# Four unread products of 512 columns after each image's part of the filter matrices, in the forward sums of a two-layer MetaFormer kernel

## The chip, the cores and the metric

The kernel runs on one core of one Trainium2 chip. A core has five engines that run side by side, each through its own queue in order: TensorE (PE in the profile; its weight loads are shown as PEld), VectorE (DVE), ScalarE (ACT), GpSimd (POOL) and SyncE (SP), which here issues the DMA transfers. TensorE writes its results to PSUM, from where ScalarE and VectorE fetch them. The metric is the device time of one execution in microseconds; the median of several runs counts.

## The reference

Two layers work on x of shape (8, 128, 32, 32). Each layer has a first part over the map and a second part over the 1024 tokens of an image, with a norm ahead of each and the input added behind it. Layer 0 has attention and then a spectral filter; layer 1 has a deformable convolution and then a mixture of experts. Only the spectral filter bears on the change. In the reference, cut to it:

```python
def _stu_conv(phi, u, n):
    Vf = jnp.fft.rfft(phi, n=n, axis=0)
    Uf_p = jnp.fft.rfft(u, n=n, axis=1)
    Uf_m = jnp.fft.rfft(u * sgn3, n=n, axis=1)
    U_plus = jnp.fft.irfft(Vf[None, :, :, None] * Uf_p[:, :, None, :], n=n, axis=1)[:, :sl]
    U_minus = jnp.fft.irfft(Vf[None, :, :, None] * Uf_m[:, :, None, :], n=n, axis=1)[:, :sl]
...
out = jnp.einsum('btkd,k,kde->bte', U_plus, s, Mpp)
out = out + jnp.einsum('btkd,k,kde->bte', U_minus, s, Mpm)
```

Each of the 8 images (u: 1024 tokens of 128 channels, normalised) is convolved along its tokens with 16 filters phi, and multiplied by one 128x128 matrix for each filter (`Mpp`, `Mpm`). That is done for four lengths of the sequence, and one of the four results is chosen by `log_weights + gumbel`.

## The kernel before

The program has four stages: attention (to about 900 us of the span), the forward sums (900 to 1038), the products in the frequency domain (to about 1400), and then the way back, the convolution and the experts.

**The forward sums** are `Spectral.forward` (L1718). They turn each image into its spectrum by products with a table of cosines and sines, `t`: 128 tokens by 4 residues by 2 pieces by 512 columns, float32, made at the start by `table` (L1704). The loop at L1794 runs over the images b = 0 to 7 and issues, in this order:

- `image(b)` (L1920): for each parity, `halves` (L1873) makes two sums in two PSUM buffers `p_half`, of two products each (L1882), so eight products of 128x128 by 128x512 for an image. ScalarE copies the second sum of each pair to `other` (L1888), and `both` (L1891) lets VectorE add and subtract the pair into `us`. After them TensorE turns the image, two times four 128x128 transposes into `p_t` (L1933), and ScalarE copies each of these to `ut` (L1934).
- the load of image b + 4 (SP), the store of `us` to `ud` and of `ut` to `utd` (L1937, L1940, SP), the load of a piece of the filter matrices for b + 3 (SP), and the norm of image b + 3 (L66): statistics on VectorE, seventeen small operations on POOL for the inverse root, and eight normalising activations on ScalarE (L105).
- `parts(b)` (L1907): four products of 512 columns in four strips of the array give this image's piece of the filter matrices in `p_a` (L1912); ScalarE (even b) or VectorE (odd b) copies it to `a`.
- at b = 1 also `spectra` (L1897), the spectrum of the filters, eight products through the same `halves`; at b = 5 and 6 the tables for the way back; and each time four steps of the setup of layer 1 (`fill`).

Everything here stands in the order in which it is written (`manual_schedule`). Each engine takes its instructions in that order and waits on semaphores for what others make.

**The PSUM buffers** are in one pool (L1694): `wide` (L1698) gives one of six buffers of 512 columns, to `p_half`, `p_a` and later `p_g`; `small` (L1701) gives one of two, to `p_t` and later `p_z`. A buffer is given again when its last reader has finished. `halves` needs four `wide` buffers for an image and `parts` one, so that TensorE can start on the next image while the earlier one waits to be fetched, until the six are used up.

**Behind the loop**, `generate` (L1944) makes the filter matrices of a chunk of frequencies from all of `a` and `v` (`p_g`, L1951), `products` (L2020) loads the spectra of all images again from `ud` (`uc`, L2030), `stationaries` (L1960) lays them out (`at`, on POOL and VectorE for the first chunk), and `apply` (L1992) multiplies (`p_z`, L2000).

Of the kernel before, what the change touches and what calls it, by code (L numbers as in the profile page):

```python
# [19 lines left out]
B = 8  # L20
# [45 lines left out]
def layer_norm_pieces(nc, pool, src, dst, eps):  # L66

    t = {}  # L70

    def stats(i):
        if i == 0:
            for name, shape in (
                ("st", [P, NT, 6]), ("mv", [P, NT, 2]), ("v", [P, NT]), ("y", [P, NT]),
                ("w", [P, NT]), ("nm", [P, NT]),
            ):
                t[name] = pool.tile(shape, F32, tag=f"lp_{name}", name=f"lp_{name}")
        nc.vector.bn_stats(t["st"][:, i, :], src()[:, i, :])
        nc.vector.bn_aggr(t["mv"][:, i, :], t["st"][:, i, :])  # L80

    def inverse(n):

        v, y, w, mv = t["v"], t["y"], t["w"], t["mv"]
        bits = [i.bitcast(I32) for i in (y, v)]
        ops = [
            lambda: nc.gpsimd.tensor_scalar(v, mv[:, :, 1], eps, None, ALU.add),
            lambda: nc.gpsimd.tensor_scalar(bits[0], bits[1], -0.5, 0x5F3759DF, ALU.mult, ALU.add),
            lambda: nc.gpsimd.tensor_scalar(v, v, -0.5, None, ALU.mult),
        ]  # L90
        ops += 3 * [
            lambda: nc.gpsimd.tensor_mul(w, y, y),
            lambda: nc.gpsimd.tensor_mul(w, w, v),
            lambda: nc.gpsimd.tensor_scalar(w, w, 1.5, None, ALU.add),
            lambda: nc.gpsimd.tensor_mul(y, y, w),
        ]
        ops += [
            lambda: nc.gpsimd.tensor_mul(t["nm"], mv[:, :, 0], y),
            lambda: nc.gpsimd.tensor_scalar(t["nm"], t["nm"], -1.0, None, ALU.mult),
        ]  # L100
        for op in ops[2 * n : 2 * n + 2]:
            op()

    def norm(i):
        nc.scalar.activation(  # L105
            dst()[:, i, :], src()[:, i, :], AF.Identity, bias=t["nm"][:, i : i + 1],
            scale=t["y"][:, i : i + 1],
        )

    return (  # L110
        [partial(stats, i) for i in range(NT)] + [partial(inverse, n) for n in range(9)]
        + [partial(norm, i) for i in range(NT)]
    )
# [656 lines left out]
class Plan:  # L770
# [18 lines left out]
    def unread(self, gap):  # L789

        return min(8, int((gap - 0.7) * 0.7 / 0.427 + 0.5)) if gap > 0.7 else 0
# [871 lines left out]
class Spectral:  # L1663
# [54 lines left out]
    def forward(self, ctx, fill, head):  # L1718


        nc = self.nc
        sb = ctx.enter_context(self.tc.tile_pool(name="s_fwd", bufs=2))
        one = ctx.enter_context(self.tc.tile_pool(name="s_one", bufs=1))
        self.sb = sb

        room = self.first.rearrange("p a b -> p (a b)")
        used = 0

        def early(size):
            nonlocal used  # L1730
            used += size
            return room[:, used - size : used]

        u = [head.x] + [one.tile([P, NT, C], F32, name=f"u{n}") for n in range(1, 4)]
        u += u

        def load(b):
            head.load(u[b], b)

        pieces = []  # L1740

        def load_parts(n):
            m = sb.tile([P, 16, C], F32, tag="m", name="m", bufs=3)
            for rows, src in ((slice(0, 64), self.M_plus), (slice(64, 128), self.M_minus)):
                nc.sync.dma_start(
                    m[rows], src[:, :, 16 * n : 16 * n + 16, :].rearrange("f k d e -> (f k) d e")
                )
            pieces.append(m)

        self.angles = [  # L1750
            [early(2 * LOW).bitcast(I32).rearrange("p (a f) -> p a f", a=2) for _ in range(2)]
            for _ in range(2)
        ]
        phi = early(HT)[0 : 2 * NF]
        load(1)
        nc.sync.dma_start(phi[0:NF], self.phi_e[:, PHI_PAD : PHI_PAD + HT])
        nc.sync.dma_start(phi[NF : 2 * NF], self.phi_o[:, PHI_PAD + 1 : PHI_PAD + 1 + HT])
        load_parts(0)
        load(2)
        load_parts(1)  # L1760
        load(3)
        mus = early(NFR * TAPS * C).rearrange("d (f i e) -> d f i e", f=NFR, i=TAPS)
        for f in range(NFR):
            nc.sync.dma_start(mus[:, f], self.M_u[f].rearrange("i d e -> d i e"))
        load_parts(2)

        self.shift = one.tile([P, 1], F32, name="shift")
        nc.gpsimd.memset(self.shift, -PI)
        waves = one.tile([P, 2], F32, name="at_wave")
        nc.gpsimd.iota(waves, pattern=[[2 * P, 2]], base=1, channel_multiplier=2,  # L1770
                       allow_small_or_imprecise_dtypes=True)
        times = early(4 * QT).rearrange("p (r q) -> p r q", r=4)
        nc.gpsimd.iota(times, pattern=[[1, 4], [4, QT]], base=0, channel_multiplier=0,
                       allow_small_or_imprecise_dtypes=True)
        t = one.tile([P, 4, 2, 2, LOW], F32, name="t")
        back = early(4 * 2 * 2 * QT).rearrange("p (r i a q) -> p r i a q", r=4, i=2, a=2)
        self.lags = early(4 * 2 * 8 * NF).rearrange(
            "p (r i j a k) -> p r i j a k", r=4, i=2, j=4, a=2
        )

        def norm(b):
            return layer_norm_pieces(nc, sb, lambda: u[b], lambda: u[b], 1e-5)

        for r in (0, 2, 1, 3):
            for i in range(2):
                self.table(t[:, r, i], head.odd, head.at[:, r, i : i + 1])
        for piece in norm(1):
            piece()
        self.scales(one)
        self.filters_turned(one, phi)  # L1790
        for piece in norm(2):
            piece()

        for b in range(B):  # L1794
            store = self.image(b, u[b], t)
            if b + 4 < B:
                load(b + 4)
            store()
            if b + 3 < B:
                load_parts(b + 3)  # L1800
                for piece in norm(b + 3):
                    piece()
            self.parts(b, pieces[b])
            if b == 1:
                self.spectra(t)
            if b == 2:
                for f in range(NFR):
                    by = self.weights[:, f : f + 1]
                    if f == 0:
                        nc.vector.tensor_scalar(self.mu, mus[:, f], by, None, ALU.mult)  # L1810
                    else:
                        nc.vector.scalar_tensor_tensor(
                            self.mu, mus[:, f], by, self.mu, ALU.mult, ALU.add
                        )
            if b in (5, 6):
                for r in range(2 * b - 10, 2 * b - 8):
                    for i in range(2):
                        self.table(back[:, r, i], times[:, r, :], waves[:, i : i + 1])
                half = slice(8 * QT * (b - 5), 8 * QT * (b - 4))
                nc.sync.dma_start(  # L1820
                    self.backd[:, half], back.rearrange("p r i a q -> p (r i a q)")[:, half]
                )
            for _ in range(4):
                next(fill, None)
        for _ in fill:
            pass
# [70 lines left out]
    def spectra(self, t):  # L1897

        for par in range(2):
            one, other = self.halves(  # L1900
                par, lambda r, i: self.lags[:, r, i].rearrange("p j a k -> p (j a k)"), t
            )
            self.both(
                lambda half, cs: self.v[:, :, LC * half : LC * half + LC, 2 * par + cs], one, other
            )

    def parts(self, n, m):  # L1907
# [325 lines left out]
```

## Time and profile before

| what | value |
|---|---|
| median of 3 runs | 1879.45 us (1876.2 to 1879.82) |
| the profiled execution | 1878.91 us, of which 1877.2 us are the span from first to last instruction |
| busy in the span: PE, DVE, ACT, POOL | 1673.7, 1385.4, 1052.6, 1156.8 us |
| mean granted TensorE clock | 0.953 of full speed |

By stage, from the windows of the trace (us busy):

| window (us) | PE | DVE | ACT | POOL | granted clock | DMA share |
|---|---|---|---|---|---|---|
| 0 to 900, attention | 851.29 | 717.14 | 576.16 | 665.39 | 0.99 | 0.04 |
| 900 to 1037.8, forward sums | 95.19 | 68.03 | 54.03 | 34.76 | 0.83 | 0.79 |
| 1037.8 to 1063.2, first filter matrices | 17.25 | 18.15 | 13.96 | 12.92 | 1.00 | 0.33 |
| 1063.2 to 1400, products | 321.51 | 187.72 | 148.86 | 124.70 | 0.98 | 0.32 |
| 1400 to 1877.2, way back, convolution, experts | 388.45 | 394.36 | 259.54 | 319.05 | 0.90 | 0.59 |

How to read the profile. A row of the timeline gives the start (us from the span's start), the length (us), the engine, the line of the kernel, the operation, what it writes and reads with its shape, how many instructions are merged, and in brackets the idle time of the engine just ahead of them with what ended it. A float32 product is shown as two rows: the eight `p_half` products of an image count as x16. In the row of slices the span is cut in 40 equal parts; each digit is a busy share in tenths, and PEclk is the clock that TensorE was granted, in tenths of full speed. "issue" in the chain of waits is time for which the profile shows no releaser.

### The profile page before, as it was taken

To read this page: it belongs to the slowest core of one execution; us is meant where nothing else is said; L and a number is where in the kernel's file an instruction comes from. 1 tells how busy PE (TensorE), PEld (TensorE's weight loads), DVE (VectorE), ACT (ScalarE), POOL (GpSimd) and SP (SyncE) were. 2 spreads that over 40 slices of the span, in tenths; PEclk is the share of its full clock that TensorE was granted. 3 is DMA by queue.
4 is the path that set the end of the run, shared out by engine and by line. 5 is a ranking of instruction groups with operands and counts; after the bars stand their busy time and mean duration, and the time that the engine had idled before them with its cause. 6 is when DMAs were issued, how large, how long until landed. Compare 5 with 4: busy or idle time off the path is not lost.

```text
span 1877.2 us, 51680 instructions
## 1 busy us (share of the span) xinstructions
PE 1673.7 (89%) x22228; PEld 1024.7 (55%) x22228; DVE 1385.4 (74%) x2107; ACT 1052.6 (56%) x1676; POOL 1156.8 (62%) x1215
## 2 busy tenths in 40 slices
PE   5999999999999999998587899999888497888788
PEld 3545555555555555554133688888665363555555
DVE  2778787888888787888545666666158888999883
ACT  3666766666666666665324455555145655666630
POOL 3778777787778777786231345445126768888740
PEclk9999999999999999999688999999898588999989
DMA  1000000000000000000678322222568775855620
GB/s 30 13 2 24 2 2 24 2 24 2 24 2 24 2 2 24 2 13 2 143 176 226 122 62 71 58 62 60 183 194 262 229 223 152 237 176 164 206 83 20
DMA packets 157999, 156.17 MB, mean 83 GB/s; under 512 B 15424, under 2 KB 136864, under 8 KB 156352
## 3 DMA queue, kind: packets, MB, share of 16 engines
q1 hardware_dynamic: 142400, 102.41, 19.3%
q0 software_dynamic: 15360, 50.34, 8.7%
q8 instruction: 177, 2.90, 0.7%
q14 instruction: 62, 0.51, 0.1%
HBM read 96.39 MB, written 56.33 MB: 81 GB/s over the span
## 4 chain that ended last, share of the span: by engine, by line
PE 55%; DVE 15%; POOL 9%; ACT 8%; issue 8%; DMA 4%; SPq 2%; DVEq 0%; POOLq 0%; ACTq 0%
PE s L598 13%; PE av L650 9%; PE p_g L1951 6%; PE z L619 5%; PE p_z L2000 5%; ACT e L603 5%; PE rb L633 3%; PE p_out L1413 3%; DVE ga L1403 3%; POOL t L612 2%; DVE g L1310 2%; DMA g<-tab,idx 2%; PE pq L554 2%; PE p_mix L1245 1%; DVE e L640 1%
## 5 line engine op out<-in xcount | busy, mean ns | idle before, releaser
L612 POOL TENSOR_TENSOR t<-e 128x1024 f32<-128x1024 f32 x256 | 608.4, 2377 | 192.4 <-ACT e L603 190.2
L603 ACT ACTIVATE e<-s 128x2048 f32<-128x2048 f32 x256 | 481.0, 1879 | 261.5 <-PE s L598 254.3
L640 DVE TENSOR_TENSOR e<-e,rb 128x2048 f32<-128x2048 f32 x256 | 568.6, 2280 | 70.0 <-PE rb L633 68.6
L598 PE MATMUL s<-q,k 32*128 32x256 f32 x4096 | 299.0, 406 | 25.4 <-ACT e L603 21.2
L650 PE MATMUL av<-e,vt 128*32 128x256 f32 x4096 | 290.6, 392 | 2.9 <-DVE e L640 1.7
L1288 POOL DMA_INDIRECT g<-tab,idx x192 | 199.4, 1038 | 133.7 <-ACT cn_m L1508 67.5
L598 PEld LDWEIGHTS s<-q,k 32*128 32x128 f32 x4096 | 187.9, 187 | 153.1 <-ACT e L603 139.6
L1295 ACT ACTIVATE g<-g,w 128x128 f32<-128x128 f32 x604 | 186.2, 390 | 61.2 <-DMA g<-tab,idx 48.9
L1976 POOL TENSOR_SCALAR at<-uc 128x256 f32<-128x256 f32 (+2 forms) x62 | 75.3, 1216 | 174.1 <-issue 86.4
L626 DVE RECIPROCAL r<-z 128x256 f32<-128x256 f32 x64 | 112.5, 1757 | 94.1 <-PE z L619 94.1
L650 PEld LDWEIGHTS av<-e,vt 128*32 128x32 f32 x4096 | 102.0, 110 | 134.9 <-issue 82.6
L1951 PE MATMUL p_g<-v,a 32*128 32x128 f32 x4096 | 159.5, 285 | 9.4 <-ACT ga L1683 3.7
L1951 PEld LDWEIGHTS p_g<-v,a 32*128 32x128 f32 x4096 | 132.4, 187 | 38.3 <-issue 23.0
L1413 PE MATMUL p_out<-ga,ew 128*128 128x512 f32 x256 | 128.0, 646 | 16.4 <-DVE ga L1403 16.3
L619 PE MATMUL z<-t,group 128*32 128x256 f32 x2048 | 122.2, 379 | 0.0
L1685 DVE COPY gb<-p_g 128x512 f32<-128x512 f32 x128 | 82.4, 685 | 46.9 <-PE p_g L1951 46.2
L1685 DVE COPY ga<-p_g 128x512 f32<-128x512 f32 x128 | 82.4, 685 | 44.0 <-PE p_g L1951 44.0
L1683 ACT COPY gb<-p_g 128x512 f32<-128x512 f32 x128 | 68.7, 589 | 69.9 <-PE p_g L1951 69.1
L1683 ACT COPY ga<-p_g 128x512 f32<-128x512 f32 x128 | 68.7, 589 | 66.7 <-PE p_g L1951 66.7
L1403 DVE TENSOR_TENSOR ga<-p_g,tc 128x2048 f32<-128x2048 f32 x32 | 73.1, 2283 | 31.6 <-PE p_g L1394 31.6
L1413 PEld LDWEIGHTS p_out<-ga,ew 128*128 128x128 f32 x256 | 50.5, 206 | 76.4 <-issue 56.5
L619 PEld LDWEIGHTS z<-t,group 128*32 128x32 f32 x2048 | 66.4, 110 | 44.2 <-issue 0.3
(309 smaller groups left out, 2378.6 us busy)
## 6 DMA issues: line engine op xcount, KB each, us to landing
tab<-hx SPq DMA_DIRECT2D x24, 512.0 KB, 5.1
tab<-hx SPq DMA_DIRECT2D x72, 128.0 KB, 5.9
ud<-us SPq DMA_DIRECT2D x8, 1024.0 KB, 6.4
uc<-ud SPq DMA_DIRECT2D x16, 512.0 KB, 4.4
yd<-zs SPq DMA_DIRECT2D x32, 256.0 KB, 3.0
ga<-yd SPq DMA_DIRECT2D x32, 256.0 KB, 3.5
xc<-in_x SPq DMA_DIRECT2D x8, 512.0 KB
x1d<-xt SPq DMA_DIRECT2D x8, 512.0 KB, 3.8
```

The lines of the kernel that those rows point to most:

```text
L598: nc.tensor.matmul(s[:, j, c, :], img["k"][rows, 2 * r + c, :], q[rows, qc * QU : (qc + 1) * QU], start=True, stop=True,)
L603: nc.scalar.activation(e.rearrange("p j c q -> p (j c q)"), s.rearrange("p j c q -> p (j c q)"), AF.Exp, scale=float(HD) ** -0.5,)
L612: nc.gpsimd.tensor_add(t, e[:, :, 0, :], e[:, :, 1, :])
L619: nc.tensor.matmul(un["z"][32 * j : 32 * j + 32, 0:QU], group, un["t", r][:, j, :], start=(r == 0), stop=(r == 3), skip_group_check=True,)
L640: nc.vector.tensor_tensor(e, e, un["rb"].unsqueeze(2).to_broadcast([P, NH, 2, QU]), ALU.mult)
L650: nc.tensor.matmul(qrt["av"][32 * j : 32 * j + 32, 0:QU], img["v"][:, 2 * r + c, P * hg + 32 * j : P * hg + 32 * j + 32], un["e", r][:, j, ...
L1288: nc.gpsimd.indirect_dma_start(out=t["g", i][:, tap].rearrange("p k c -> p (k c)"), out_offset=None, in_=rows, in_offset=bass.IndirectOffs ...
L1295: nc.scalar.activation(t["g", i][:, tap, k, :], t["g", i][:, tap, k, :], AF.Identity, scale=t["w"][:, i, tap, k : k + 1],)
L1413: nc.tensor.matmul(t["out"], self.ew[:, first + e, :], xg[:, e, :], start=(first + e == 0), stop=(first + e == NE - 1), skip_group_check=True,
L1683: self.nc.scalar.copy(dst, src)
L1685: self.nc.vector.tensor_copy(dst, src)
L1951: nc.tensor.matmul(banks[j][:, i * P : (i + 1) * P], self.a[rows, 4 * n + i, :], self.v[rows, ch].rearrange("p f k -> p (f k)"), start=Tru ...
```

## The change

Behind `parts(b)` the loop calls a new function for each image but the last. It takes one of the two `small` buffers and writes four products to it, with the identity as the fixed operand and the first 512 columns of the table `t` as the moving one. Nothing reads the result.

```diff
@@ -1801,6 +1801,8 @@
                 for piece in norm(b + 3):
                     piece()
             self.parts(b, pieces[b])
+            if b + 1 < B:
+                self.unread(t)
             if b == 1:
                 self.spectra(t)
             if b == 2:
@@ -1902,6 +1904,14 @@
             )
             self.both(
                 lambda half, cs: self.v[:, :, LC * half : LC * half + LC, 2 * par + cs], one, other
+            )
+
+    def unread(self, t):
+        p = self.small("p_idle")
+        for _ in range(4):
+            self.nc.tensor.matmul(
+                p, self.ident, t[:, 0, 0].rearrange("p a f -> p (a f)"), start=True, stop=True,
+                skip_group_check=True,
             )
 
     def parts(self, n, m):
```

## The prediction

> **What bounds the kernel now.** I read the page's slices first, to find where TensorE is neither busy nor at full clock:
>
> ```profile
> PE   5999999999999999998587899999888497888788
> PEclk9999999999999999999688999999898588999989
> DMA  1000000000000000000678322222568775855620
> ```
>
> The change sits in slices 19 to 22 (a slice is 46.9 us). There TensorE is idle for part of the time, its granted clock falls to 0.6, and the DMA engines are the busiest of the span. The windows view gives this stage, from 900 to 1037.8 us: PE 95.2 of 137.8 us busy, DVE 68.0, ACT 54.0, POOL 34.8, clock 0.83. No engine fills the stage; a chain that passes from engine to engine sets its length. The chain of waits follows it over the stage: the seventeen small POOL operations of a layer norm, then "issue" of about 10 us, then POOL again, once each 15 us. ScalarE's part of the timeline shows one such round:
>
> ```profile
> 1013.58 3.18 ACT L105 ACTIVATE u<-u,lp_nm,lp_y 128x128 f32<-128x128 f32 x8 [9.55 <-POOL lp_nm L99]
> 1016.67 0.56 ACT L1683 COPY a<-p_a 128x512 f32<-128x512 f32 x1
> 1017.14 1.06 ACT L1888 COPY other<-p_half 128x512 f32<-128x512 f32 x2
> 1018.09 1.07 ACT L1934 COPY ut<-p_t 128x512 f32<-128x512 f32 x2
> ```
>
> ScalarE waits for POOL's layer norm of image b+3, normalises it, and only then copies what TensorE made for image b long before (`other`, then `ut`). VectorE's `us` for image b waits for `other`, and the statistics of the next norm are queued behind `us`: `us` starts at 937.41, 952.46, 987.98, 1002.62 and 1017.75, so a round takes 15.0 us. TensorE has spare time in these rounds. Behind image 5 no norm is left, and then TensorE is last:
>
> ```profile
> 1007.89 1.04 PE L1933 MATMUL p_t<-ident,u 128*128 128x128 f32 x8
> 1008.86 1.07 PE L1912 MATMUL p_a<-m,by 128*32 128x512 f32 x8
> 1017.29 9.46 PE L1882 MATMUL p_half<-t,u 128*128 128x512 f32 x16 [7.36 <-ACT a L1683]
> 1026.59 1.04 PE L1933 MATMUL p_t<-ident,u 128*128 128x128 f32 x8
> 1027.55 1.07 PE L1912 MATMUL p_a<-m,by 128*32 128x512 f32 x8
> 1028.55 7.13 PE L1882 MATMUL p_half<-t,u 128*128 128x512 f32 x16
> ```
>
> The reader is to see two things: images 6 and 7 run back to back (1017.29 to 1037.5), and the release ahead of them is a ScalarE copy at 1016.67. ACT's second `other` copy of image 7 starts at 1035.78, as image 7's products end (1035.68). From there the last `us`, its store (SP, 1037.84), the load of `uc` (SP, 1045.60), POOL's `at` (1049.72) and the first `p_z` (1063.20) follow each other. So a delay of image 7's last product is a delay of everything after it.
>
> **The change, part by part.** It adds 7 groups (images 0 to 6) of 4 products, 128x128 by 128x512 in float32, on TensorE. They are never read, so no other engine gets an instruction, and no DMA is added. Two costs follow: the products, and the wait that their output buffer brings.
>
> *Price of a group.* The product has the shape of a `p_half` product (8 of them show as 16 rows). Two rows of four:
>
> ```profile
> 961.54 3.60 PE L1882 MATMUL p_half<-t,u 128*128 128x512 f32 x8
> 967.12 5.40 PE L1882 MATMUL p_half<-t,u 128*128 128x512 f32 x8 [1.98 <-ACT other L1888]
> ```
>
> So 3.60 us at full clock and 5.40 at a reduced one; all seven are 25.2 us of work at full clock.
>
> *The wait.* `p_idle` takes a buffer of the two that `p_t` uses. Both hold the turned image b until ScalarE has copied it, and the built program puts a wait for ScalarE on the first product of each group. The group thus starts when the first `ut` copy of image b has ended, 0.58 us after the start of the `ut` pair (or after `p_a`, if that is later). Behind the waiting product, in TensorE's queue, stand all products of image b+1 (and of `spectra`, for b = 1), so these no longer run ahead. The times of before, with 3.60 for a group, 7.13 for an image's eight `p_half` products and 1.82 for `p_t` and `p_a` (1028.55 to 1037.5 is 8.95, less 7.13), at full clock:
>
> - b = 0: `ut` copied 938.34, group to 941.9, image 1 to 949.1. ScalarE's second `other` copy of image 1 comes at 952.3: 3.2 us spare. TensorE has stood idle for 11 us here; the losses seen after its idle gaps are 1.4 to 3.1 us (8.49 and 9.46 for 7.13; 12 rows in 8.42 for 5.35), so even that just fits.
> - b = 1: starts 953.4, group to 957.0, `spectra` to 964.1. ScalarE wants these at 966.5: hidden. Image 2 then follows without the gap of 1.98 and without the 1.8 us of low clock (the 5.40 row): to 971.2, where it ended at 972.5. ScalarE and VectorE waited there for TensorE (VectorE 1.04 us), so this is a **gain of 1.0 us** for all that follows.
> - b = 2: starts 973.1 behind `p_a`, image 3 to 983.8, wanted from 986.4: hidden.
> - b = 3: `ut` at 987.9 (with the gain), image 4 to 998.6, wanted at 1001.5: hidden.
> - b = 4: `ut` at 1002.6, image 5 to 1013.3, wanted at 1016.6: hidden.
> - b = 5: `ut` at 1018.67 less 1.0 = 1017.67; group to 1021.27; image 6 to 1028.4. It ended at 1026.7: **not hidden**. The idle 7.36 us ahead of image 6 can't take the group, since `ut` is copied only at its end.
> - b = 6: `p_t`, `p_a` to 1030.2, group to 1033.8 (the `ut` copies of image 6 run beside `p_a`, so no wait), image 7 to 1040.95: **not hidden**, nothing of TensorE is idle here.
>
> So image 7 ends at 1040.95 against 1035.68: **+5.3 us**. It contains 7.2 of added products and 1.4 for starting behind `ut` and not `a` (1018.67 for 1017.29), less 1.0 gained at image 2 and 2.3 because image 6 starts behind products instead of behind an idle gap (7.13 for 9.46).
>
> *The clock at b = 5.* Whether the group there starts at full clock is open: TensorE is idle from about 1015.1 to 1017.7, 2.6 us. [...] The rows differ among themselves: 2.50 us idle before 1002.64 cost nothing (12 rows in 5.42), but 1.98 us before 967.12 cost 1.8. By the second row the sum is +7.1. [...]its two rows are equally near: I take the middle, 0.9, hence **+6.2 us**, and keep both ends.
>
> After the stage nothing is added and the order on every engine stays, so I take the whole delay to reach the end. The profiled execution took 1878.91 us (span 1877.2 and 1.7 around it): 1878.91 + 6.2 = **1885.1 us**. It lies 0.5 below the median of the runs, within their spread of 3.6.
>
> **The rivals.**
>
> *The warm clock pays (not slower).* The unread products keep TensorE busy, and the losses of clock vanish everywhere: image 1 3.1, `spectra` 2.5, image 2 1.8, image 4 1.7, image 6 2.3, in all 11.4 us, against 7.2 of unread products at the tail: 1874.7. It decides from the point where more than 7.2 us of these losses lie on the path. For it: the clock of 0.83. Against it: only images 2 and 6 are waited for, 4.1 us; at image 1, `spectra` and image 4 the rows show ScalarE coming from POOL, not TensorE. Chance 0.04.
>
> *The tail hides most of it (no change).* Another chain, VectorE's `ga` and `gb` copies or the `uc` load, sets the first `p_z`, or the wait on `ut` costs nothing; then one group's worth minus the gain is left, +2.6 or less: 1881.5 at most. Against it: both chains begin after image 7. Chance 0.12.
>
> *The new wait closes a ring.* With `ut` to group to image to `other`, a round of TensorE takes 1.5 + 3.6 + 7.1 = 12.2 us of the 15.0. With a clock loss of 3.1 in each round it is 15.3, and rounds 0, 3 and 4 would come late by up to a microsecond each, on top of 7.1: some +9.5, 1888.4. Against it: after gaps of 2 to 3 us the loss was 1.8 at most. Chance 0.12.
>
> *TensorE is the bound throughout.* All seven groups count: +25.2, 1904.1. Against it: the 42 us in which TensorE is idle in the stage. Chance 0.02.
>
> **How the numbers follow.** The forecast has 0.70. Its own range is +5.3 to +7.1, plus 1.0 if the gain at image 2 fails, with the spread of the runs (about 1.8 to each side): 1882.4 to 1888.8. I stretch it to 1882.0 and 1889.5 for the ring. What can't be told from no change is 0.2%, 3.8 us. Slower: forecast, ring and bound throughout, 0.84, less a little for a forecast at its lower end, 0.82. Same 0.14, faster 0.04.
>
> **What would show it.** Right: the first `p_idle` of each group waits for ACT `ut`; `us` still starts each 15.0 us up to image 5; image 6's eight products take 7.1 and not 9.5; image 7's last product ends 5 to 7 us later, and so does the first `p_z`. Wrong: rounds longer than 15.0 us (the ring), or the first `p_z` moving by less than image 7 does (the tail hides it), or a first `p_z` that comes earlier than 1063.2 (the clock pays).

## The result, and the profile after

| | before | after |
|---|---|---|
| median of 7 runs | 1878.1 us (1873.83 to 1880.55) | 1884.6 us (1882.32 to 1887.31) |
| ratio to before, 95% interval | | 1.0043 [1.0028, 1.0058] |
| span of the profiled execution | 1877.2 us | 1882.8 us |
| windows of the stage: PE busy, granted clock | 95.19 us of 900 to 1037.8, 0.83 | 113.09 us of 900 to 1043.4, 0.89 |

The changed kernel is slower by 6.5 us by the medians (1.0035; the recorded ratio is 1.0043); the forecast was 6.2 us. Two rows of the page of after, the slices of TensorE:

```profile
PE   5999999999999999997499899999888497888788
PEclk6999999999999999999699999999999687999989
```

In slices 20 to 22 (counted from 0) the clock digits are 9 9 9, where they were 8 8 9. TensorE is busier and has a better clock there, and the kernel is slower. TensorE's timeline of after shows why, from image 5's group of unread products to image 7 (L1884 is the old L1882; all lines behind the new call are 2 or 10 further down):

```profile
1014.42 3.70 PE L1912 MATMUL p_idle<-t,ident 128*128 128x512 f32 x8 [0.97 <-ACT ut L1944]
1017.96 7.03 PE L1884 MATMUL p_half<-t,u 128*128 128x512 f32 x16
1024.82 1.04 PE L1943 MATMUL p_t<-ident,u 128*128 128x128 f32 x8
1025.79 1.06 PE L1922 MATMUL p_a<-m,by 128*32 128x512 f32 x8
1026.79 3.70 PE L1912 MATMUL p_idle<-t,ident 128*128 128x512 f32 x8
1030.32 7.03 PE L1884 MATMUL p_half<-t,u 128*128 128x512 f32 x16
```

Image 6 takes 7.03 us instead of 9.46: the granted clock over these products is 1.00, where it was 0.75. But it starts behind a group that waited for the `ut` copy, and a second group stands between it and image 7. ScalarE in the same execution:

```profile
1012.83 1.06 ACT L1890 COPY other<-p_half 128x512 f32<-128x512 f32 x2
1013.78 1.06 ACT L1944 COPY ut<-p_t 128x512 f32<-128x512 f32 x2
...
1034.01 0.58 ACT L1890 COPY other<-p_half 128x512 f32<-128x512 f32 x1 [2.06 <-PE p_half L1884]
1037.44 0.58 ACT L1890 COPY other<-p_half 128x512 f32<-128x512 f32 x1 [2.85 <-PE p_half L1884]
```

At image 5 (1012.83) its two `other` copies follow each other without waiting for TensorE; at image 7 it waits 2.06 and 2.85 us for TensorE.

Executions differ by some microseconds ahead of the stage (first `p_phi` from 903.9 to 909.5 us in the traces below) and behind it. So I measure from the first `p_phi` row, in us: the **stage length** runs to the end of image 7's last `p_half` row, the **first p_z** to the start of the first `p_z` row.

| kernel | stage length | first p_z | ratio to before, 95% interval |
|---|---|---|---|
| before | 126.25 | 153.77 | |
| after | 130.98 | 158.37 | 1.0043 [1.0028, 1.0058] |
| after_again | 132.63 | 160.04 | 1.0035 [1.0014, 1.0055] |
| only_last | 129.61 | 157.36 | 1.002 [1.0009, 1.0032] |
| only_five | 130.84 | 158.58 | 1.0011 [0.9996, 1.0025] |
| first_five | 122.62 | 151.76 | 1.0012 [0.9997, 1.0027] |
| first_five_again | 123.12 | 155.30 | 1.0004 [0.9989, 1.0019] |
| wait_only | 126.60 | 154.09 | 1.0 [0.9985, 1.0014] |
| no_wait | 128.34 | 155.75 | 1.001 [0.9992, 1.0029] |
| double | 147.34 | 174.76 | 1.0125 [1.0101, 1.0149] |
| two_places | 123.27 | 154.53 | 1.0006 [0.9992, 1.002] |
| three_places | 123.28 | 155.27 | 1.0005 [0.9991, 1.0019] |
| before_again | 126.29 | 153.79 | |

The first p_z of after is 4.6 us later, in a second execution 6.3 us; 0.2% of the whole time is 3.8 us, so most of the other rows are below what the times alone can tell.

### The profile page after: what moved, and what is told of

It reads as the page before. It is cut to its first block, busy times and chain, and to the rows that moved or that the text cites. A ratio compares the mean times of both kernels' runs of the same rounds, so it can differ in the third digit from the quotient of the medians.

```text
span 1882.8 us, 51781 instructions
## 1 busy us (share of the span) xinstructions
PE 1681.2 (89%) x22284; PEld 1029.7 (55%) x22284; DVE 1388.3 (74%) x2107; ACT 1052.3 (56%) x1676; POOL 1155.4 (61%) x1215
## 4 chain that ended last, share of the span: by engine, by line
PE 52%; DVE 19%; POOL 8%; issue 8%; ACT 7%; DMA 3%; SPq 2%; DVEq 0%; ACTq 0%; POOLq 0%
PE s L598 13%; PE av L650 9%; PE p_g L1961 6%; PE z L619 5%; PE p_z L2010 5%; ACT e L603 5%; DVE ga L1403 3%; PE rb L633 3%; POOL t L612 2%; DVE g L1310 2%; PE p_out L1413 2%; PE pq L554 2%; DVE e L640 1%; DVE zs L2022 1%; POOL g L1288 1%
## 5 line engine op out<-in xcount | busy, mean ns | idle before, releaser
L650 PE MATMUL av<-e,vt 128*32 128x256 f32 x4096 | 286.8, 387 | 5.3 <-DVE e L640 4.0
L1413 PE MATMUL p_out<-ga,ew 128*128 128x512 f32 x256 | 132.1, 664 | 19.3 <-DVE ga L1403 19.3
```

The lines of the kernel that those rows point to most:

```text
L650: nc.tensor.matmul(qrt["av"][32 * j : 32 * j + 32, 0:QU], img["v"][:, 2 * r + c, P * hg + 32 * j : P * hg + 32 * j + 32], un["e", r][:, j, ...
L1413: nc.tensor.matmul(t["out"], self.ew[:, first + e, :], xg[:, e, :], start=(first + e == 0), stop=(first + e == NE - 1), skip_group_check=True,
```

## The experiments

My theory was that of the prediction: of the seven groups only those of images 5 and 6 are on the path. The rivals are that every group costs its share, and that the wait for `ut` costs and not the work.

**The group of image 6 alone**

```diff
-            if b + 1 < B:
+            if b == 6:
                 self.unread(t)
```

> The group of four unread products stands behind image 6 alone. I measure the stage from the first p_phi row to the end of image 7's last p_half row: 126.25 us before, 130.98 with all seven groups. Theory (only the two groups of the tail cost, each its own length): image 6 as before (9.5 us from a cold start), then 3.6 us of group ahead of image 7: stage 129.8 us, ratio to before 1.002. Rival (each of the seven groups adds its share, 4.7 / 7 = 0.7 us): stage 126.9 us, ratio 1.0004.

The stage is 129.61 us, 3.4 more than before, and the ratio 1.002. TensorE's timeline of this run:

```profile
1011.69 9.44 PE L1884 MATMUL p_half<-t,u 128*128 128x512 f32 x16 [7.33 <-ACT a L1683]
...
1022.93 3.70 PE L1912 MATMUL p_idle<-t,ident 128*128 128x512 f32 x8
1026.47 7.03 PE L1884 MATMUL p_half<-t,u 128*128 128x512 f32 x16
```

Image 6 starts behind 7.33 us of idle time and needs 9.44 us, as before; one group follows and nothing takes it up. A seventh of the cost (0.7 us, ratio 1.0004) is excluded: narrowly by the times, whose interval begins at 1.0009, and clearly by the stage.

**The groups of images 0 to 4 alone** (`if b < 5:` in the same place)

> The groups stand behind images 0 to 4 alone. Theory (these five are hidden behind ScalarE's wait for POOL, and the one behind image 1 takes away the low clock of image 2): stage 125.2 us against 126.25 before, ratio 0.9995, image 6 still about 9.5 us. Rival (each of the seven adds its share): 126.25 + 5 x 0.7 = 129.6 us, ratio 1.002.

The stage is 122.62 us, 3.6 shorter than before: the five groups are hidden, and more. I expected image 6 to start at a low clock; it took 7.13 us (granted clock 1.00 from 1015 to 1025 us); image 5 is done later, and only 1.23 us of idle time lie ahead of image 6, where it was 7.36. But the time didn't fall (1.0012; the traced execution was the fastest of 20, 1871.17 us for a median of 1877.89), so I ran it again.

> The kernel with the groups of images 0 to 4 once more, since its stage was 3.6 us shorter in the trace (122.6) and its time not. Theory (image 6 starts at full clock in some executions only): stage 122.6 or 125, ratio 0.998 to 1.000. Rival (the five groups cost outside of the stage): ratio 1.001 or more, and more than 814 us from the first p_z to the end.

The stage is 123.12 us, and the first p_z comes at 155.30, later than before. What was won up to image 7 is gone by then. TensorE behind image 7 in the two runs, first_five and then first_five_again:

```profile
1035.40 1.38 PE L1961 MATMUL p_g<-v,a 32*128 32x128 f32 x36 [2.71 <-DVE a L1685]
1037.27 1.27 PE L1961 MATMUL p_g<-v,a 32*128 32x128 f32 x32 [0.49 <-ACT ga L1683]
```

```profile
1036.46 2.50 PE L1961 MATMUL p_g<-v,a 32*128 32x128 f32 x36 [2.69 <-DVE a L1685]
1039.25 2.19 PE L1961 MATMUL p_g<-v,a 32*128 32x128 f32 x32 [0.28 <-ACT ga L1683]
1041.69 2.24 PE L1961 MATMUL p_g<-v,a 32*128 32x128 f32 x32 [0.25 <-ACT ga L1683]
1044.18 2.17 PE L1961 MATMUL p_g<-v,a 32*128 32x128 f32 x32 [0.25 <-ACT ga L1683]
1046.66 1.32 PE L1961 MATMUL p_g<-v,a 32*128 32x128 f32 x32 [0.32 <-ACT ga L1683]
```

In both, VectorE is now last: `p_g` waits 2.7 us for its copy to `a` (0.91 before), which gives back half of the 3.6. In the second, the granted clock falls (0.59 from 1035 to 1040 us, 0.50 to 1045, 0.88 to 1050, against 1.00 in first_five), and the first four `p_g` groups take 2.2 to 2.5 us each instead of 1.3 to 1.4, some 3 us in all, which gives back more than the rest. That was neither of the two things I had set against each other: the groups cost nothing themselves, but the microseconds won before image 7 run into the next limits.

**The wait without the work**

```diff
-        for _ in range(4):
+        for _ in range(1):
             self.nc.tensor.matmul(
-                p, self.ident, t[:, 0, 0].rearrange("p a f -> p (a f)"), start=True, stop=True,
+                p[:, 0:16], self.ident, t[:, 0, 0, 0, 0:16], start=True, stop=True,
```

> Each of the seven groups is one product of 16 columns instead of four of 512: the wait for ScalarE's ut copy stays, the work goes. Theory (the wait alone costs the later start of image 6, 1.4 us, less up to 1.0 at image 2): stage 126.7 to 127.7 us, ratio 1.000 to 1.001. Rival (the wait, not the products, is the cost): stage 131 us, ratio 1.0025 or more.

```profile
1015.94 0.39 PE L1912 MATMUL p_idle<-t,ident 128*128 128x16 f32 x2 [2.91 <-ACT ut L1944]
1016.18 8.81 PE L1884 MATMUL p_half<-t,u 128*128 128x512 f32 x16
```

The stage is 126.60 us, 0.35 more than before and just below what I expected, and the ratio 1.0. The wait alone isn't the cost.

**The work without the wait.** The same four products, written to `p_a`'s buffer just ahead of the products that overwrite it:

```diff
-            self.parts(b, pieces[b])
+            self.parts(b, pieces[b], t if b + 1 < B else None)
...
-    def parts(self, n, m):
+    def parts(self, n, m, t, count=4):
...
         pa = self.wide("p_a")
+        if t is not None:
+            for _ in range(count):
+                nc.tensor.matmul(
+                    pa, self.ident, t[:, 0, 0].rearrange("p a f -> p (a f)"), start=True, stop=True,
+                    skip_group_check=True,
+                )
```

> All seven groups of four stay, but are written to the p_a buffer just ahead of the products that use it, so they wait for nothing. Theory: the group of image 5 falls into the idle time ahead of image 6, the group of image 6 keeps its 3.6 us: stage 127.5 (image 6 at full clock) to 129.8 us (image 6 from a cold start, 9.5 us), ratio 1.001 to 1.002. Rival (the work costs wherever it stands): stage 131 us.

```profile
1008.66 3.60 PE L1913 MATMUL p_a<-t,ident 128*128 128x512 f32 x8
1012.19 1.07 PE L1918 MATMUL p_a<-m,by 128*32 128x512 f32 x8
1015.55 7.13 PE L1882 MATMUL p_half<-t,u 128*128 128x512 f32 x16 [2.30 <-ACT a L1683]
```

Image 5's group now lies in the idle time, 2.30 us of which are left, and image 6 takes 7.13 us. The stage is 128.34 us, 2.6 less than after with the same products. The difference at the tail is larger still, since here image 2 gains nothing: TensorE is idle for 4.46 us ahead of its second half, which then takes 6.16 us (5.40 before), and image 2's products end 1.0 us later than before. From there to the end of image 7's products it takes 64.2 us, before 63.2 and in after 69.3. So image 5's group costs because of the two together: the wait carries the work out of the idle time and puts it ahead of image 6.

**The group of image 5 alone** (`if b == 5:`). This run, three_places and before_again fell on another chip, where the kernel before took 1921.67 us; their ratios are to that.

> The group of four stands behind image 5 alone. Theory (it waits for ScalarE's ut copy, so it starts 1.4 us later than image 6 did, and after some 8.8 us of idle time at a low clock, 5.4 to 6.5 us, with image 6 at 7.1 behind it): stage 130.7 to 131.8 us against 126.25 before, more than the group of image 6 alone (129.6). Rival (a group adds its 3.6 us, wherever it is not hidden): stage 129.8 us.

```profile
1017.13 5.32 PE L1912 MATMUL p_idle<-t,ident 128*128 128x512 f32 x8 [8.80 <-ACT ut L1944]
1022.29 7.03 PE L1884 MATMUL p_half<-t,u 128*128 128x512 f32 x16
1031.12 7.13 PE L1884 MATMUL p_half<-t,u 128*128 128x512 f32 x16
```

The stage is 130.84 us, as expected: alone, this group costs 4.6 us, more than image 6's 3.4. The loss behind the idle time (8.80 us here) is not the reason. It has passed from image 6 to the group: the group takes 5.32 us, where groups behind no idle time take 3.70, and image 6 follows in 7.03 us, where it took 9.46. The reason is the later start. TensorE begins 1.86 us later than image 6 did (109.72 us behind the first `p_phi`, before 107.86), the group adds 5.16, and image 6 saves 2.44. With the other groups around it, in the first execution of after, TensorE has been idle for 0.97 us only, and the group takes 3.70. The time agrees weakly: the first p_z is 4.8 us later, which would be 1.0025, the upper end of the interval.

**Eight products in a group**

> Eight unread products in a group instead of four. Theory (a group is hidden only as far as the rounds have room, and in full on the path at images 5 and 6): 7.1 us more at the tail, 3.4 more at spectra and image 2, and one to two more at images 1 and 5, whose last product now comes 2 us later than ScalarE wants it: stage 141 to 144 us against 130.98, ratio to before 1.009 to 1.011. Rival (the groups of images 0 to 4 are hidden whatever their length): only the tail grows, stage 138.1 us, ratio 1.008.

The stage is 147.34 us and the ratio 1.0125, both above what I expected. In TensorE's timeline there is no idle time left from 937.5 us to the end of image 7:

```profile
1010.25 7.13 PE L1912 MATMUL p_idle<-t,ident 128*128 128x512 f32 x16
1017.22 7.03 PE L1884 MATMUL p_half<-t,u 128*128 128x512 f32 x16
1024.09 1.04 PE L1943 MATMUL p_t<-ident,u 128*128 128x128 f32 x8
1025.06 1.06 PE L1922 MATMUL p_a<-m,by 128*32 128x512 f32 x8
1026.05 7.13 PE L1912 MATMUL p_idle<-t,ident 128*128 128x512 f32 x16
```

A round of TensorE's own work, 1010.25 to 1026.05, is now 15.8 us, more than the 15.0 of the round. I had added up single delays and not the queue: TensorE has become the bound of every round. With four products the work is 3.5 us less, 12.3 us, and fits.

**The changed kernel again**

> The changed kernel once more, for a second trace. Theory (the cost is in the stage, the rest differs from run to run): stage 131 us again, or up to 1.8 more where the group of image 5 starts at a low clock; first p_z 158 to 160 us behind the first p_phi; ratio 1.003 to 1.004. Rival (the stages behind are slowed as well): first p_z to the end again 4 us longer than the 814.0 of before.

```profile
1014.74 5.40 PE L1912 MATMUL p_idle<-t,ident 128*128 128x512 f32 x8 [2.67 <-ACT ut L1944]
1019.98 7.03 PE L1884 MATMUL p_half<-t,u 128*128 128x512 f32 x16
```

This execution has the other price of image 5's group, 5.40 us behind 2.67 us of idle time, and a stage 1.65 us longer. In the two traces the price goes with the groups ahead. In the first execution image 4's group had lost time, at a granted clock of 0.67:

```profile
999.32 5.40 PE L1912 MATMUL p_idle<-t,ident 128*128 128x512 f32 x8 [2.17 <-ACT ut L1944]
```

So image 5 was done later, and only 0.97 us of idle time were left ahead of its group. In the second execution image 3's group lost time (5.14 us), image 4's did not (3.70), and the idle time ahead of image 5's was 2.67 us again. From the first p_z to the end it took 815.2 us, the first execution of after 818.1, before 814.0; the other runs on such chips lie between 809.4 and 817.2, so nothing marks the 4 us more of the first execution as a property of the change.

**Towards a faster kernel.** The clock losses that count are at image 2 (5.40 us for 3.60) and image 6 (9.46 for 7.13), so I put products without a wait only there (`no_wait`'s code, ten at b = 1 and eight at b = 5).

> Unread products only where TensorE is idle and its next products are waited for: ten behind image 1 and eight behind image 5, written to the p_a buffer ahead of its own products, so without a wait. Theory (the low clock of image 2 and image 6 is on the path, 1.0 and 2.3 us): stage 123 us against 126.25 before, ratio 0.998 to 0.999. Rival (such products cost time outside of the stage, or the clock there doesn't matter): ratio 1.000 or more.

The stage is 123.27 us, 3.0 shorter, but `p_g` waits 2.69 us for VectorE, and three of its groups take 2.2 us (granted clock 0.68 from 1035 to 1040 us, 0.64 to 1045), much as in first_five_again: first p_z 154.53, ratio 1.0006. I took the 2.7 us of idle time ahead of `p_g` for the cause of the low clock and filled it with two more products at b = 7.

> As with unread products at images 1 and 5 alone, and two more ahead of image 7's piece of the filter matrices, which fill most of the 2.7 us that TensorE stood idle ahead of the first p_g there. Theory (that idle time let the clock of the first four p_g groups fall to half in two of three traces, 2.5 us a group instead of 1.8, which gave the gain of image 6 back): the first p_g groups at full clock, first p_z 151.5 to 152 us behind the first p_phi (153.8 before, 154.5 with the two places), ratio 0.998 to 0.9995. Rival (the fall of the clock there has another cause): 154.5 us or more, ratio 1.000 or more.

```profile
1037.00 1.38 PE L1957 MATMUL p_g<-v,a 32*128 32x128 f32 x36 [0.98 <-DVE a L1685]
1039.60 2.21 PE L1957 MATMUL p_g<-v,a 32*128 32x128 f32 x32 [1.21 <-ACT ga L1683]
```

That idea fell: with 0.98 us of idle time ahead of the first group and 1.21 ahead of the second the loss comes all the same, from the second group on (2.21, 2.23 and 1.99 us, then 1.32). No version here is faster than before by what can be measured. As a control, the kernel before on the same chip:

> The kernel before once more, for a second trace. Theory (the rounds repeat from execution to execution): stage 126.3 us within 0.5, first p_z 153.8 us behind the first p_phi; the stretches ahead of and behind it differ by some us. Rival: the stage itself differs by more than 2 us, and the traces of the other runs can't be compared with one of before.

Stage 126.29 and first p_z 153.79 us: the stage repeats within 0.1 us, on a chip where the whole execution takes 42 us more.

## Why the prediction was right

- **The number.** That 6.5 us came out for 6.2 is in part luck. The interval of the ratio is 5.3 to 10.9 us, and 6.2 was the middle of two ends, of which each traced execution shows one. In the profiled execution of after the first `p_z` is 4.6 us later; the span is 5.6 us longer because the stretch ahead of the stage was 3.1 us shorter and the one behind the first `p_z` 4.1 us longer, which are differences such as any two executions show.
- **What bounds the stage.** Rounds of 15 us that end with ScalarE behind POOL's norm, TensorE last only behind image 5: shown. In after the starts of `us` are 15.0, 14.6 and 15.1 us apart, as before. Five groups alone don't lengthen the stage (122.62 and 123.12), one at image 6 does by 3.4, one at image 5 by 4.6.
- **Price of a group.** 3.60 or 5.40 us were taken; the rows of `p_idle` are 3.70 and 5.40, and 5.5 to 6.6 behind 11 us of idle time at image 0, where it was hidden as reckoned.
- **The gain at image 2.** In after, image 1's `us` to image 3's takes 34.4 us (949.36 to 983.73), before 35.5 (952.46 to 987.98): 1.15 us for the 1.0 forecast. Image 2's products are one row now:

```profile
960.74 7.35 PE L1884 MATMUL p_half<-t,u 128*128 128x512 f32 x16
```
- **The tail.** The sum was +5.3 at full clock and +7.1 at low clock; measured are +4.7 and +6.4. Both ends occur, in one execution each, and both sums were about 0.6 too large: 0.2 from the larger gain at image 2, and 0.35 because groups and images follow each other more closely (22.93 us from image 5's group to image 7's end, where I had 23.28).
- **The clock at b = 5.** Two rows of before give the two ends: behind 2.50 us of idle time nothing was lost (granted clock 1.00 over the row), behind 1.98 us 1.8 us were (0.67). Both prices are in the later traces too: behind 2.17, 2.39, 2.42, 2.47 and 2.67 us of idle time a group took 5.14 to 5.40 us, behind 2.38 us 3.70, behind 0.97 us and less always 3.70. The length of the gap alone doesn't decide: at image 2 some 2.0 us (1.97 to 2.15) cost 1.8 us in each trace where the groups don't reach it, at image 5 some 2.5 us (2.48 to 2.51) cost nothing in each. So the prediction was right to keep both ends open, but its middle (0.9 us for the clock) is a case that neither trace of after shows: the clock cost this group nothing in one (3.70 us) and 1.7 us in the other (5.40). What separates the two was not shown.
- **Nothing is taken up behind the stage.** Image 7 to the first p_z takes 27.5 us before and 27.4 in both executions of after. The chain that the prediction named (store, `uc`, `at`) is not alone there. Before, POOL's `at` ends last and releases the first `p_z`, behind 1.95 us of idle time. In after `at` is done 1.7 us ahead of it, and `p_z` comes 1.77 us behind the last of thirteen `p_g` groups. Both chains begin behind image 7, so the delay passes either way. In the other direction this doesn't hold: a stage that ends earlier is not a kernel that ends earlier.
- **The rivals.** The warm clock does pay at the two places named (image 2, 1.15 us; image 6, 7.03 us for 9.46), but less than the two groups cost. The ring and TensorE as the bound come with eight products (15.8 us of work for a round of 15.0), not with four (12.3).

## What to carry to other kernels

Work that TensorE did in idle time was free here only as long as it ended before the next thing that was waited for (stage 122.62 us with the five groups of images 0 to 4 and 129.61 with image 6's alone, before 126.25); check it at each round, and at the last rounds first, where the chain that hid it has ended. The output buffer of such work decided when it could run: with a buffer that ScalarE still had to empty, the group at image 5 missed the idle time that was meant for it (alone, it started behind 8.80 us of it). Before work is added in every round, add up the engine's whole queue for one round and compare it with the round's length. Where an idle gap of 2 to 3 us stands ahead of products that are waited for, reckon with both prices: here such a gap cost nothing in some traces and 1.8 us in others.

## What was not expected of the hardware

The first `p_g` groups lost time for some 7 to 10 us in three of the four traces in which image 7 ended 3 us earlier (2.0 to 2.5 us a group for 1.3 to 1.4; the granted clock of first_five_again was 0.50 from 1040 to 1045 us), once with only 0.98 and 1.21 us of idle time ahead, and in none of the others, not even behind `double`, where TensorE had been busy for 120 us without a gap. And the same idle time of 2.4 us was followed by a full clock in one execution (2.38 us, 3.70 us for a group, granted clock 1.00) and by a loss in another (2.39 us, 5.14 us), both of the same kernel.

Side by side, with the length of the same products where they lose nothing:

| place | idle time ahead, us | products behind it, us | without a loss, us |
|---|---|---|---|
| before, image 2, second half | 1.98 | 5.40 | 3.60 |
| before, image 5, six products | 2.50 | 5.42 | 5.35 (three quarters of 7.13) |
| after, group of image 3 | 2.38 | 3.70 | 3.70 |
| after_again, group of image 3 | 2.39 | 5.14 | 3.70 |
| first_five, first `p_g` | 2.71 | 1.38 | 1.38 |
| first_five_again, first `p_g` | 2.69 | 2.50 | 1.38 |
| three_places, first and second `p_g` | 0.98 and 1.21 | 1.38 and 2.21 | 1.38 and 1.27 |
| double, first `p_g` | 1.00 | 1.38 | 1.38 |

At the first `p_z` it is the same: behind 1.77 or 1.78 us of idle time its row took 1.25 or 1.26 us in three traces (first_five, first_five_again, three_places) and 1.69 to 1.94 us in five (after, after_again, no_wait, two_places, double).

So in these traces the length of the idle time does not tell which price follows. They don't show what does: no run moved an idle gap by itself to test it.
